# A graph layer on one core: order by sets of two units, 24 groups gathered wholly by TensorE, and another way to h's bf16 parts

## The chip, the cores and the metric

The kernel runs on one core of one Trainium2 chip. The metric is the device time of one execution in microseconds (us). Five engines work side by side, each through its own queue in order: TensorE (PE, with its weight loads as PEld), VectorE (DVE), ScalarE (ACT), GpSimd (POOL), and SyncE (SP), which here only issues DMA transfers.

## What is computed

One layer of a graph network with 6250 nodes of 64 values and 206250 edges, sorted by target node:

```
h   = relu(layernorm(x))                      # 6250 x 64
msg = relu(h[src] + edge_attr)                # 206250 x 64
agg = segment_sum(msg, dst)                   # 6250 x 64
out = x + relu((h + agg) @ W1 + b1) @ W2 + b2
```

## The kernel before

**Groups.** The edges are cut into 269 groups of 768: 128 partitions with G = 6 edges each (the last group has fewer). Because edges are sorted by target, all targets of a group lie in a window of W = 32 nodes. For each group the kernel needs the 768 rows h[src], adds the edge rows `ea`, takes the relu (`messages`, L589 to L605), and multiplies by a one-hot matrix `oh` of the edges' places in the window (`one_hot`, L577; `window_sum`, L607, two column halves of TensorE at a time). The result, 64 values by 32 nodes, is added into `z`, which holds h plus agg with the 64 values as partitions (`sum_into_z`, L573). Blocks of 512 nodes that are complete go through the two dense layers (`hidden`, `result`, `store`, L626 to L653).

**Two ways to h[src].** Half of a group's rows (three of its six columns) are gathered by GpSimd, one indirect DMA of 128 rows for each column (`gather`, L200, from the DRAM copy `h_rows`). The other half, a *unit* of 3 columns by 128 edges, comes from TensorE: h stands in SBUF as `hp`, 128 partitions by 49 node rows, as three bf16 parts whose sum is h in f32. TensorE first moves the wanted rows into slots (`slots_of`, L488, with the one-hot `found`) and then from the slots to the edges (`pick`, L508, with the one-hot `backs`), accumulating over `ea`, which ScalarE has put into the PSUM bank before (`room`, L517). A *whole* group has both halves from TensorE, so two units and no gather. The first F0 = 5 groups are gathered wholly, and the first RAW = 3 of them from x itself, with a layer norm of their own (`norm_edges`, L543), because h isn't ready by then.

**Units and sets.** The list `UNITS` (L65) has 276 units: 264 for groups 5 to 268, and 12 second ones for the whole groups (`WHOLE`, L64). Two units are a *set* (138), three sets a *chunk* (46). For every set, `find` (L460) makes `found` by two long compares and a short one on VectorE; `back_far`, `back` and `back_near` (L472 to L486) make `backs`, six compares of which VectorE does five and ScalarE the sixth (as a distance and a relu); `slots_out` (L505) evacuates the slots as bf16. For every chunk, the ranking steps `rank_at`, `rank_count`, `rank_of`, `rank_marks`, `rank_holds`, `rank_fits`, `rank_turn` and `source` (L278 to L347) sort the edges of six units into slots and write two small lists to DRAM, which SP loads again, spread over all partitions (`source_load`, `spot_load`).

**Order.** The order is written by hand; nothing reorders it. `half(u)` (L678) emits one unit: window sum of unit u - 1, room and slots for the next set (three pairs of slots), pick of unit u + 1, the messages of unit u, its one-hot, compares for later sets, the sum into z of unit u - 2, blocks, and at fixed distances the chunk steps. So TensorE's stream for a unit is W (window sum), S (slots), P (pick). `beats` are TensorE instructions that a gather waits for, so that gathers don't run ahead. Every 16 groups, `window_start` (L439) loads window positions into VectorE's registers.

**Opening.** The layer norm runs in four pieces over the 49 rows (`ln_head`, `ln_rows`, L356 to L377). After each piece TensorE transposes it into z (`ln_turn`, L379, evacuated by ScalarE). `slots_of_edges` (L741) computes all places in windows; it needs one small product by TensorE (L747). `ln_parts` (L389) makes the three bf16 parts of h with ScalarE and VectorE; it is a generator, and `fill` hands out its steps between the first five groups.

Of the kernel before, what the change touches and what calls it, by code (L numbers as in the profile page):

```python
# [21 lines left out]
G = 6  # L22
# [39 lines left out]
HEAD, PERIOD = 2 * RG - 1, 4 * RG - 1  # L62
assert (NG + 1 - F0 - HEAD) % PERIOD == 0
WHOLE = [F0 + RG - 1] + list(range(F0 + HEAD + 2 * RG - 1, NG + 1, PERIOD))  # L64
# [17 lines left out]
def kernel(  # L82
# [78 lines left out]
    nc.gpsimd.iota(from0, pattern=[[1, S], [0, H]], base=0, channel_multiplier=0, allow_small_or_imprecise_dtypes=True)  # L161
    ident_b = const.tile([P, P], BF16, name="ident_b")
    nc.vector.tensor_copy(ident_b, ident)
    ones_b = const.tile([P, P], F16, name="ones_b")
# [73 lines left out]
    code = const.tile([P, NCH, CC], F32, name="code")  # L238
    assert PARTS <= S

    def from0_all(n):
        return from0[:, :n].unsqueeze(1).to_broadcast([P, RG, n, H])
# [4 lines left out]
    def stretches(t_sb, c0, c1):  # L247

        n, g0 = (HEAD, F0) if c0 == 0 else (PERIOD, F0 + HEAD + (c0 - 2) // 4 * PERIOD)
# [5 lines left out]
    def places(c0, c1):  # L255
# [5 lines left out]
        own = lnp.tile([P, n, CC], F32, name="own", bufs=1)  # L261
        m, parts = stretches(src_sb, c0, c1)
        for src, w, gs in parts:
            nc.vector.tensor_copy(own.rearrange("p c s -> p (c s)")
                                  .rearrange("p (e w g j) -> p e w g j", w=2, g=m, j=H)[:, :, w, gs], src)
# [6 lines left out]
        nc.vector.scalar_tensor_tensor(part[:, c0:c1], off, float(RR), third, op0=ALU.add, op1=ALU.add)  # L272
        nc.vector.tensor_scalar(code[:, c0:c1], part[:, c0:c1], float(STEP), float(BIAS), op0=ALU.mult, op1=ALU.add)
# [4 lines left out]
    def rank_at(c):  # L278
        ats[c] = rank.tile([P, RG, PARTS, H], F16, name="at")
        nc.vector.tensor_tensor(ats[c], over(part[:, c], PARTS), from0_all(PARTS), ALU.is_equal)  # L280
# [12 lines left out]
    def rank_of(c):  # L293
# [7 lines left out]
        nc.vector.tensor_tensor(spot_i[c], ranks[c], code[:, c], ALU.add)  # L301
# [9 lines left out]
    def rank_holds(c):  # L311
        holds[c] = rank.tile([P, RG, S, H], F16, name="holds")
        nc.vector.tensor_tensor(holds[c], over(ranks[c], S), from0_all(S), ALU.is_equal)  # L313
# [41 lines left out]

    def ln_head(r, n):  # L356
# [32 lines left out]
    def ln_parts(r, m, h):  # L389
        hv = hp[:, r:r + m]  # L390
        rest = lnp.tile([PP, m, D], F32, name="rest")
        nc.scalar.copy(hv[:, :, 0], h)
        yield
        nc.vector.tensor_tensor(rest, h, hv[:, :, 0], ALU.subtract)
        nc.scalar.copy(hv[:, :, 1], rest)
        yield
        nc.vector.tensor_tensor(hv[:, :, 2], rest, hv[:, :, 1], ALU.subtract)
# [62 lines left out]

    def find(k, b):
# [3 lines left out]
        nc.vector.tensor_scalar(found[k][:, b * PARTS:b * PARTS + n].rearrange("p m i s -> p (m i s)"),  # L465
                                sources[k][:, :n * 2 * S], nodes_of[:, b:b + 1], None, op0=ALU.is_equal)

    far = const.tile([P, 1], F32, name="far")
    nc.vector.tensor_scalar_mul(far, ids[:, Q - 1:], -1.0)
    dists = {}  # L470

    def back_far(k):  # L472
        dists[k] = rank.tile([P, 2 * H * P], BF16, name="dist", bufs=1)
        nc.scalar.activation(dists[k], spots[k].bitcast(I16), AF.Abs, bias=far)  # L474

    def back_near(k):
        nc.scalar.activation(backs[k][:, Q - 1].rearrange("p t s -> p (t s)"), dists.pop(k), AF.Relu,  # L477
                             bias=ones[:, 0:1], scale=-1.0)
# [64 lines left out]
    def norm_edges(xg):  # L543
        s = work.tile([P, G], F32, name="raw_s")
# [5 lines left out]
        fill()  # L550
        v = work.tile([P, G], F32, name="raw_v")
        nc.vector.tensor_reduce(v, sq, AX.X, ALU.add)
        nc.scalar.activation(v, v, AF.Sqrt, bias=eps_sb, scale=1.0 / D)
        fill()
# [5 lines left out]
    pick_banks = [psum.tile([P, H + 1, 4, D], F32, name=f"pick{i}", bufs=1) for i in range(2)]  # L560

# [28 lines left out]
    def messages(u):  # L590
# [3 lines left out]
        if g < RAW:  # L594
            norm_edges(xg)
# [78 lines left out]

    def half(u):
        g = group_of(u)
        k, i = divmod(u, 2)
        first = ((0, 2), (6, 8))[i]  # L678
        later = ((4,), (10,))[i]
        now = is_set(k + 1)  # L680
        if is_first(u):
            enter(g + AHEAD, beats[-G + H:])
        if i == 0:
            if is_set(k + 3):
                source_load(k + 3)
        elif is_set(k + 3):
            spot_load(k + 3)
        window_sum(u - 1)
        if u + 1 < U:
            room(u + 1)  # L690
        if now:
            for n0 in first:
                begun = slots_of(k + 1, n0)
                slots_out(k + 1, n0)
                if n0 == first[0]:
                    beats.append(begun)
            for n0 in later:
                beats.append(slots_of(k + 1, n0))
        if u + 1 < U:
            beats.append(pick(u + 1, range(H)))  # L700
        messages(u)
        if now:
            for n0 in later:
                slots_out(k + 1, n0)
# [223 lines left out]
```

## Time and profile before

| | |
|---|---|
| Median of 3 runs | 1082.63 us (1082.12 to 1085.3) |
| The profiled execution, its own time | 1080.78 us |
| Its span | 1079.1 us |
| Granted TensorE clock, mean | 0.974 |
| Matmuls (PE) | 23185 |
| VectorE instructions | 2686 |
| ScalarE instructions | 1979 |

The profile is of one execution. A row of a timeline has the start, the time from the first start to the last end, the engine, the line of the kernel, the operation, its tiles (out<-in), shape and count; in brackets stands the idle time ahead of it and what ended it. A row of a group has the count, the busy time of all, the mean of one in ns, and the idle time ahead of them. Matmuls overlap, so their pace is read from start to start.

### The profile page before, as it was taken

What the parts mean: (1) busy time and instruction counts of PE and PEld (TensorE: products, weight loads), DVE (VectorE), ACT (ScalarE), POOL (GpSimd) and SP (SyncE); (2) the same over time, 40 slices, a digit from 0 to 9 for tenths busy, and PEclk for the clock granted to TensorE, in tenths of its full rate; (3) what the DMA queues carried; (4) which work ended last, traced back from release to release, by engine and by line L of the source; (5) the groups of instructions that cost most, each with busy time, mean ns of one, the idle gap of its engine ahead of it and who ended that gap; (6) DMA issues with size and microseconds to landing.
All of it is one profiled execution on the core that took longest, in us unless ns stands there. A gap on an engine that the chain in (4) does not pass through costs nothing.

```text
span 1079.1 us, 55140 instructions
## 1 busy us (share of the span) xinstructions
PE 994.9 (92%) x23185; PEld 865.5 (80%) x23185; DVE 960.5 (89%) x2686; ACT 940.6 (87%) x1979; POOL 793.9 (74%) x798
## 2 busy tenths in 40 slices
PE   3159999999999999999999999999999999999997
PEld 2148888888878888888888888888888888888885
DVE  8869889898998998998999898998999898998984
ACT  6459889899989998898998998998998998998985
POOL 7677777777777777777777777777777777777740
PEclk9659999999999999999999999999999999999998
DMA  6445566565655665665665656565656665655650
GB/s 207 126 117 150 164 164 187 141 178 158 188 143 150 180 190 143 170 169 165 163 174 149 184 157 165 155 199 156 161 148 187 164 170 154 185 158 161 167 132 10
DMA packets 115098, 172.36 MB, mean 160 GB/s; under 512 B 28444, under 2 KB 83613, under 8 KB 114845
## 3 DMA queue, kind: packets, MB, share of 16 engines
q1 hardware_dynamic: 89752, 143.03, 43.7%
q0 software_dynamic: 25088, 25.74, 13.5%
q8 instruction: 184, 3.01, 1.1%
q14 instruction: 70, 0.57, 0.2%
q10 hardware_dynamic: 4, 0.01, 0.0%
HBM read 164.85 MB, written 3.84 MB: 156 GB/s over the span
## 4 chain that ended last, share of the span: by engine, by line
PE 76%; DVE 10%; issue 5%; DMA 4%; ACT 3%; POOL 1%; DVEq 1%; SPq 0%; ACTq 0%
PE pick L513 34%; PE half L497 26%; PE half L612 10%; DVE backs L484 2%; DVE found L465 2%; DVE ea L600 2%; DMA xg<-h_rows,src_sb 2%; PE rows L339 2%; PE rows L642 1%; PE rows L631 1%; PE rows L287 1%; POOL xr L204 1%; DMA x<-in_x_dram 1%; DVE oh L581 1%; PE rows L285 1%
## 5 line engine op out<-in xcount | busy, mean ns | idle before, releaser
L204 POOL DMA_INDIRECT xg<-h_rows,src_sb x754 | 759.4, 1007 | 231.6 <-issue 105.2
L513 PE MATMUL pick<-picked,backs 128*128 128x192 bf16 x4968 | 459.9, 247 | 1.1 <-ACT pick L522 1.1
L513 PEld LDWEIGHTS <-backs 128*128 128x128 bf16 x4968 | 397.5, 98 | 45.1 <-issue 43.6
L506 ACT CAST picked<-half 128x384 bf16<-128x384 f32 x828 | 370.4, 480 | 54.3 <-PE half L497 47.2
L497 PE MATMUL half<-hp,found 128*32 128x192 bf16 x14352 | 352.8, 248 | 7.5 <-DVE found L465 4.9
L497 PEld LDWEIGHTS <-found 128*32 128x32 bf16 x14352 | 286.6, 97 | 22.2 <-issue 5.1
L484 DVE TENSOR_SCALAR backs<-spots,ids 128x768 bf16<-128x768 int16 x690 | 255.8, 419 | 0.0
L600 DVE TENSOR_REDUCE ea<-pick 128x192 f32<-128x576 f32 x276 | 206.8, 749 | 21.6 <-PE pick L513 19.7
L465 DVE TENSOR_SCALAR found<-sources,nodes_of 128x1536 bf16<-128x1536 int16 (+1 forms) x414 | 206.1, 525 | 0.1
L612 PEld LDWEIGHTS half<-oh,msg 128*64 128x64 f32 x3224 | 121.7, 138 | 62.0 <-issue 27.4
L522 ACT COPY pick<-ea 128x576 f32<-128x576 f32 x264 | 170.4, 646 | 0.0
L612 PE MATMUL half<-oh,msg 128*64 128x32 f32 x3224 | 152.4, 227 | 13.5 <-DVE z L575 10.8
L602 ACT ACTIVATE msg<-ea 128x384 f32<-128x384 f32 (+2 forms) x281 | 146.3, 521 | 10.7 <-DVE ea L600 7.2
L477 ACT ACTIVATE backs<-dist,ones 128x768 bf16<-128x768 bf16 x138 | 131.7, 954 | 0.3 <-ACT dist L474 0.3
L474 ACT ACTIVATE dist<-spots,far 128x768 bf16<-128x768 int16 x138 | 131.4, 952 | 0.0
L575 DVE TENSOR_TENSOR z<-z,half 128x32 f32 x281 | 50.9, 181 | 73.2 <-ACT picked L506 43.5
L581 DVE TENSOR_TENSOR oh<-slot,slots 128x192 f32<-128x192 int16 (+2 forms) x281 | 94.5, 336 | 1.0 <-PE half L612 1.0
L597 DVE TENSOR_TENSOR ea<-ea,xg 128x192 f32<-128x192 f32 x252 | 87.4, 347 | 0.7 <-issue 0.7
L285 PE MATMUL rows<-at,upper 128*128 128x432 f16 x46 | 16.4, 358 | 21.7 <-DVE at L280 19.7
L339 PE MATMUL rows<-holds,marks 128*96 128x96 f16 x276 | 25.8, 231 | 11.4 <-DVE holds L313 5.0
L291 ACT CAST before<-rows 128x432 f16<-128x432 f32 x46 | 23.9, 519 | 14.3 <-PE rows L287 14.3
L344 ACT CAST source<-rows 24x64 int16<-24x64 f32 x138 | 28.1, 203 | 9.5 <-PE rows L339 4.4
(107 smaller groups left out, 435.1 us busy)
## 6 DMA issues: line engine op xcount, KB each, us to landing
sources<-source_row SPq DMA_DIRECT2D x138, 384.0 KB
ea<-in_edge_attr_dram SPq DMA_DIRECT2D x268, 192.0 KB
spots<-spot_rows SPq DMA_DIRECT2D x138, 192.0 KB
xg<-h_rows,src_sb POOLq DMA_INDIRECT x754
xb<-in_x_dram SPq DMA_DIRECT2D x12, 128.0 KB
out_dram<-o SPq DMA_DIRECT2D x12, 128.0 KB
h_rows<-x SPq DMA_DIRECT2D x3, 384.0 KB
dst_sb<-in_dst_main_dram SPq DMA_DIRECT2D x1, 804.0 KB
```

Of the source, the lines that this page charges most:

```text
L204: it = nc.gpsimd.indirect_dma_start(out=xg[:, j, :], out_offset=None, in_=rows[:, :], in_offset=bass.IndirectOffsetOnAxis(ap=idx[:, j:j + ...
L465: nc.vector.tensor_scalar(found[k][:, b * PARTS:b * PARTS + n].rearrange("p m i s -> p (m i s)"), sources[k][:, :n * 2 * S], nodes_of[:, b ...
L474: nc.scalar.activation(dists[k], spots[k].bitcast(I16), AF.Abs, bias=far)
L477: nc.scalar.activation(backs[k][:, Q - 1].rearrange("p t s -> p (t s)"), dists.pop(k), AF.Relu, bias=ones[:, 0:1], scale=-1.0)
L484: nc.vector.tensor_scalar(backs[k][:, q].rearrange("p t s -> p (t s)"), spots[k].bitcast(I16), ids[:, q:q + 1], None, op0=ALU.is_equal)
L497: last = nc.tensor.matmul(ps[j * S:(j + 1) * S, u], found[k][:, m, i, :], hp[:, min(m, RR - 1)].rearrange("p t d -> p (t d)"), start=(b == ...
L506: nc.scalar.copy(picked[k][:, n0:n0 + 2], halves.pop((k, n0)))
L513: last = nc.tensor.matmul(ps[:, u, :3].rearrange("p t d -> p (t d)"), backs[k][:, q, i * H + u, :], picked[k][:, i * Q + q], start=False, ...
L522: nc.scalar.copy(picks[u][:, :H, :3], parts)
L600: nc.vector.tensor_reduce(ea[:, c0:c0 + H], picks.pop(u)[:, :H, :3].rearrange("p j t d -> p j d t"), AX.X, ALU.add)
L602: nc.scalar.activation(msg[:, lo:hi], ea[:, lo:hi], AF.Relu)
L612: last = nc.tensor.matmul(pa[i * D:(i + 1) * D], msg[:, j, :], oh[:, j, :], start=(j < lo + 2), stop=(j >= hi - 2))
```

## The change

- **24 whole groups.** `WHOLE` has every eleventh group instead of every 23rd: 24 instead of 12. That is 288 units, 144 sets and 48 chunks, and 718 gathers instead of 754 in the loop.
- **Order by sets.** `half` has two shapes. For the first unit of a set: window sum of unit u - 1, room, the first three pairs of slots with their evacuations, pick of u + 1, messages, room for u + 2, one-hot, both sums into z, blocks, the last three compares of `backs`, the first of `found`. For the second: pick of u + 1, messages, the other three pairs of slots, window sum of u - 1, one-hot, the first three compares of `backs`, the second of `found`. So TensorE's stream for a set is W, W, S, P, P, S instead of W, S, P, W, S, P. The chunk steps stand one unit earlier; those of TensorE fall between the two P.
- **Compares.** All six compares of `backs` are VectorE's; the short one of `found` is ScalarE's, as a distance and a relu.
- **h's bf16 parts.** TensorE subtracts: into PSUM goes h by the identity (f32), less the first part by a negative identity (bf16); ScalarE evacuates the difference as the second part, TensorE takes that off too, and ScalarE evacuates the third. This is done within the layer norm, piece by piece.
- **Transposes.** All four `ln_turn` stand behind the layer norm and the parts, ahead of `slots_of_edges`.
- **Raw groups.** Their layer norm is done step by step for the three groups together.
- **Places.** The constant of `code` is part of `part`, so `code` goes; the casts of the later chunks' source numbers are ScalarE's, within the layer norm.

```diff
-HEAD, PERIOD = 2 * RG - 1, 4 * RG - 1
-WHOLE = [F0 + RG - 1] + list(range(F0 + HEAD + 2 * RG - 1, NG + 1, PERIOD))
+HEAD = PERIOD = 2 * RG - 1
+WHOLE = list(range(F0 + RG - 1, NG + 1, PERIOD))
...
-        nc.vector.tensor_scalar(code[:, c0:c1], part[:, c0:c1], float(STEP), float(BIAS), op0=ALU.mult, op1=ALU.add)
...
-    def ln_parts(r, m, h):
-        hv = hp[:, r:r + m]
-        rest = lnp.tile([PP, m, D], F32, name="rest")
-        nc.scalar.copy(hv[:, :, 0], h)
-        yield
-        nc.vector.tensor_tensor(rest, h, hv[:, :, 0], ALU.subtract)
-        nc.scalar.copy(hv[:, :, 1], rest)
-        yield
-        nc.vector.tensor_tensor(hv[:, :, 2], rest, hv[:, :, 1], ALU.subtract)
+    def mid_piece(i, r, m, h):
+        hv = hp[:, r:r + m]
+        nc.scalar.copy(hv[:, :, 0], h)
+        for ps, rows_of in pieces(i, r, m):
+            nc.tensor.matmul(ps, ident, h[:, rows_of].rearrange("p r d -> p (r d)"), start=True, stop=False)
+            nc.tensor.matmul(ps, less_b, hv[:, rows_of, 0], start=False, stop=True)
+        flat = pick_banks[i % 2].rearrange("p j t d -> p (j t) d")
+        nc.scalar.copy(hv[:, :, 1], flat[:, :m])
+
+    def low_piece(i, r, m, h):
+        hv = hp[:, r:r + m]
+        for ps, rows_of in pieces(i, r, m):
+            nc.tensor.matmul(ps, less_b, hv[:, rows_of, 1], start=False, stop=True, skip_group_check=True)
+        flat = pick_banks[i % 2].rearrange("p j t d -> p (j t) d")
+        nc.scalar.copy(hv[:, :, 2], flat[:, :m])
...
+        if b < BB:
+            nc.vector.tensor_scalar(to, sources[k][:, :n * 2 * S], nodes_of[:, b:b + 1], None, op0=ALU.is_equal)
+        else:
+            dist = rank.tile([P, J * 2 * S], BF16, name="dist", bufs=1)
+            nc.scalar.activation(dist, sources[k][:, :n * 2 * S], AF.Abs, bias=last_node)
+            nc.scalar.activation(to, dist, AF.Relu, bias=ones[:, 0:1], scale=-1.0)
...
-        for q in range(q0, min(q1, Q - 1)):
+        for q in range(q0, q1):
...
+        if i == 0:
             window_sum(u - 1)
             room(u + 1)
+            if is_set(k + 1):
+                slots_by(k + 1, (0, 2, 4))
             beats.append(pick(u + 1, range(H)))
+            messages(u)
+            if u + 2 < U:
+                room(u + 2)
+            one_hot(u)
+            for v in (u - 2, u - 1):
+                sum_into_z(v)
+                blocks_behind(v)
             if is_set(k + 1):
                 back(k + 1, 3, Q)
             if is_set(k + 2):
                 find(k + 2, 0)
                 find(k + 2, BB)
         else:
+            if u + 1 < U:
+                beats.append(pick(u + 1, range(H)))
+            messages(u)
+            if is_set(k + 1):
+                slots_by(k + 1, (6, 8, 10))
+            window_sum(u - 1)
+            one_hot(u)
             if is_set(k + 2):
                 back(k + 2, 0, 3)
+                find(k + 2, 1)
...
         if len(rows) > 1:
-            ln_turn(*rows[-2])
+            low_piece(len(rows) - 2, *rows[-2])
+        if rows:
+            mid_piece(len(rows) - 1, *rows[-1])
...
+        if r == CUTS[3]:
+            own = places_own(2, NCH)
     rows.append(ln_rows(*heads[-1]))
-    ln_turn(*rows[-2])
-    split = [ln_parts(*r) for r in rows]
+    low_piece(len(rows) - 2, *rows[-2])
+    mid_piece(len(rows) - 1, *rows[-1])
+    low_piece(len(rows) - 1, *rows[-1])
+    for row in rows:
+        ln_turn(*row)
...
     slots_of_edges()
-    ln_turn(*rows[-1])
...
+    for step in (raw_head, raw_var, raw_rows):
+        for g in range(RAW):
+            step(g)
```

More of the change, by code (lines that the diff above doesn't have):

```diff
@@ L354, in next_half @@
         return half_banks[halves_made[0] % 3]
+    pick_banks = [psum.tile([P, H + 1, 4, D], F32, name=f"pick{i}", bufs=1) for i in range(2)]
     def ln_head(r, n):
@@ L464, in find @@
         n = PARTS if b < BB else J
[L465 to L478, printed above, removed]
+        to = found[k][:, b * PARTS:b * PARTS + n].rearrange("p m i s -> p (m i s)")
+        if b < BB:
+            nc.vector.tensor_scalar(to, sources[k][:, :n * 2 * S], nodes_of[:, b:b + 1], None, op0=ALU.is_equal)
+        else:
+            dist = rank.tile([P, J * 2 * S], BF16, name="dist", bufs=1)
+            nc.scalar.activation(dist, sources[k][:, :n * 2 * S], AF.Abs, bias=last_node)
+            nc.scalar.activation(to, dist, AF.Relu, bias=ones[:, 0:1], scale=-1.0)
     def back(k, q0, q1):
@@ L541, in span, with raw_head @@
         return first_col(g), G
-    def norm_edges(xg):
-        s = work.tile([P, G], F32, name="raw_s")
+    raw = {}
+    def raw_head(g):
+        xg = taken[g][1]
+        s = work.tile([P, G], F32, name="raw_s", bufs=RAW)
         nc.vector.tensor_reduce(s, xg, AX.X, ALU.add)
@@ L673, in is_set, with slots_by @@
         return 0 <= k < KS
+    def slots_by(k, n0s):
+        for n0 in n0s:
+            last = slots_of(k, n0)
+            slots_out(k, n0)
+            if n0 != n0s[1]:
+                beats.append(last)
     def half(u):
@@ L758 @@
     heads, rows = [], []
-    places(0, 2)
+    places(0, 2, places_own(0, 2))
     rank_at(0)
@@ L787 @@
         enter(g)
-    places(2, NCH)
+    places(2, NCH, own)
     for k in (0, 1):
@@ L818 @@
     sum_into_z(-LAG - 1)
-    while split:
-        fill()
     ln_stack.close()
```

120 lines of the change are left out of this document (51 added, 69 removed).

## The prediction

> **What bounds the kernel now.** I read the page's busy shares and its chain first, then one window over the whole edge loop, then TensorE's timeline inside it.
>
> ```profile
> span 1079.1 us, 55140 instructions
> ...
> PE 994.9 (92%) x23185; PEld 865.5 (80%) x23185; DVE 960.5 (89%) x2686; ACT 940.6 (87%) x1979; POOL 793.9 (74%) x798
> ...
> PE 76%; DVE 10%; issue 5%; DMA 4%; ACT 3%; POOL 1%; DVEq 1%; SPq 0%; ACTq 0%
> ```
> ```profile
> 78.00:1065.00 987.00, 962.18 (x22873) 841.87 (x22871) 896.28 (x2536) 894.16 (x1896) 736.52 (x731) 1.00 0.60 162
> ```
> The columns of the window are its length and the busy time of PE, PEld, DVE, ACT, POOL. The edge loop (unit 0's window sum to the last unit's) takes 987 of 1079 us; TensorE idles 24.8 us of it, VectorE 90.7. So three things count: TensorE's work per set, how near VectorE comes to it, and the 78 us ahead of the loop.
>
> **The loop on TensorE.** Three units, L513 being the pick P, L612 the window sum W, L497 the slots S:
>
> ```profile
> 502.29 1.66 PE L513 MATMUL pick<-picked,backs 128*128 128x192 bf16 x18
> 503.79 0.56 PE L339 MATMUL rows<-holds,marks 128*96 128x96 f16 x6
> 504.27 0.54 PE L612 MATMUL half<-oh,msg 128*64 128x32 f32 x12
> 504.74 1.26 PE L497 MATMUL half<-hp,found 128*32 128x192 bf16 x52
> 505.93 1.66 PE L513 MATMUL pick<-picked,backs 128*128 128x192 bf16 x18
> 507.52 0.54 PE L612 MATMUL half<-oh,msg 128*64 128x32 f32 x12
> 507.99 1.26 PE L497 MATMUL half<-hp,found 128*32 128x192 bf16 x52
> 509.18 1.66 PE L513 MATMUL pick<-picked,backs 128*128 128x192 bf16 x18
> 510.68 0.35 PE L285 MATMUL rows<-at,upper 128*128 128x432 f16 x1
> 510.86 0.47 PE L287 MATMUL rows<-at,ones_b 128*128 128x288 f16 x2
> 511.26 0.42 PE L612 MATMUL half<-oh,msg 128*64 128x32 f32 x6
> 511.61 1.26 PE L497 MATMUL half<-hp,found 128*32 128x192 bf16 x52
> ```
> From start to start: a unit is 505.93 to 509.18 = 3.25 us, a set 6.50. P takes 1.59 ahead of W but 1.50 ahead of L339 or L285, so leaving P for the 64-column W costs 0.09. W with 12 matmuls takes 0.47, with 6 (half a group) 0.35: 0.12 for 6, so 0.25 for 12 and 0.22 for coming and going.
>
> The new order of a set is W W S P P S: six changes of kind become four. P P takes 1.50 + 1.59 = 3.09. The two S take 2.38, if P to S and S to W, which this trace doesn't show, cost what the shown changes do. The first W of the pair takes at least 0.25 (no change) and at most 0.35; with 0.30 the pair is 0.77. The set: 3.09 + 2.38 + 0.77 = 6.24 (6.19 to 6.29; with two free changes about 6.0). The Trainium skill, TensorEngine Tiling (Array Packing), Key Properties, says that changing the tiling mode drains TensorE; by that rule both unseen changes drain, the upper values hold, and the 0.09 above agrees. Now 288 units are 144 sets: 144 x 6.24 = 899 against 138 x 6.50 = 897: +2 (-5 to +9). Twenty-four more units have the short W: -3.
>
> Ranking steps (46 chunks, then 48) now all stand between two P's. Today L285/L287 add 0.58 - 0.09, L339 0.48 - 0.09, and L325 0.16:
>
> ```profile
> 84.42 0.22 PE L325 MATMUL rows<-ident_b,spot_i 128*18 128x128 bf16 x1
> 84.58 0.54 PE L612 MATMUL half<-oh,msg 128*64 128x32 f32 x12
> ```
> Sum 1.04. Between P's the change W would have needed isn't shared any more: 0.50 + 0.40 + 0.25 = 1.15 (1.0 to 1.25). Per chunk +0.1, and two chunks more: +7 (0 to +12). TensorE in all: +6 (-8 to +18), so 968 us busy.
>
> **The loop on VectorE.** Here the sixth compare of backs comes from ScalarE, and the short compare of found goes to it.
>
> ```profile
> L484 DVE TENSOR_SCALAR backs<-spots,ids 128x768 bf16<-128x768 int16 x690 | 255.8, 419 | 0.0
> L600 DVE TENSOR_REDUCE ea<-pick 128x192 f32<-128x576 f32 x276 | 206.8, 749 | 21.6 <-PE pick L513 19.7 <-ACT msg L602 0.9
> L465 DVE TENSOR_SCALAR found<-sources,nodes_of 128x1536 bf16<-128x1536 int16 x276 | 174.6, 633 | 0.1
> L465 DVE TENSOR_SCALAR found<-sources,nodes_of 128x256 bf16<-128x256 int16 x138 | 42.5, 308 | 0.0
> L477 ACT ACTIVATE backs<-dist,ones 128x768 bf16<-128x768 bf16 x138 | 131.7, 954 | 0.3 <-ACT dist L474 0.3
> L474 ACT ACTIVATE dist<-spots,far 128x768 bf16<-128x768 int16 x138 | 131.4, 952 | 0.0
> L602 ACT ACTIVATE msg<-ea 128x256 f32<-128x256 f32 x1 | 0.4, 403 | 0.0
> ```
> backs: 864 - 690 = 174 more, 255.8/690 = 0.37 each: +64. Short found: -42.5. Twelve more reduces +9, twelve more long founds +7.6; two chunks of about 2.5 us +5; the other small ones cancel. VectorE +44: 940 us. ScalarE loses 263 us of 768-wide passes and gains 288 of about 0.45, 130 us, so from 894 it falls to about 760 and gives no bound. Every 16 groups VectorE also loads window starts into registers and stands still:
>
> ```profile
> 250.87 0.19 DVE L575 TENSOR_TENSOR z<-z,half 128x32 f32 x1 [2.14 <-ACT dist L474]
> PE half L612 <- DVE z L575: 9.2, 12, 1.4
> ```
> The first row is one such stop (2.14 us idle; the releaser named was long done), the second what TensorE waits behind them today: 9.2 us in all, since VectorE runs ahead by over 1 us. 940 + 15 x 2.1 = 972: VectorE's own floor passes TensorE's 968. In the new order these stops stand between z and the three backs that the second P waits for, and behind them in VectorE's queue are found, the next reduce, and so ScalarE's room and relu. I let them cost 9 us more than now, and take 9 off for waits that go because ranking's inputs are a set old: TensorE's idle stays 25. Loop: 968 + 25 = 993, **+6** (-8 to +30).
>
> **Ahead of the loop.** VectorE's way to the loop, with the rows that price the new steps:
>
> ```profile
> 14.83 1.02 DVE L372 SCALAR_TENSOR_TENSOR x<-x,ln_v 128x832 f32<-128x832 f32 x1
> 26.61 0.96 DVE L372 SCALAR_TENSOR_TENSOR x<-x,ln_v 128x768 f32<-128x768 f32 x1
> 28.92 1.83 DVE L748 SCALAR_TENSOR_TENSOR slot<-dst_sb,rows 128x1608 int16<-128x1608 int32 x1 [0.87 <-PE rows L747]
> 68.27 1.34 DVE L465 TENSOR_SCALAR found<-sources,nodes_of 128x1536 bf16<-128x1536 int16 x3
> L394 DVE TENSOR_TENSOR rest<-x,hp 128x768 f32<-128x768 f32 x3 | 2.9, 968 | 0.2 <-ACT hp L392 0.2
> L397 DVE TENSOR_TENSOR hp<-rest,hp 128x768 bf16<-128x768 f32 x3 | 2.9, 952 | 0.9 <-ACT hp L395 0.9
> L392 ACT CAST hp<-x 128x768 bf16<-128x768 f32 x3 | 2.4, 815 | 0.0
> L363 ACT ACTIVATE ln_sq<-x 128x768 f32<-128x768 f32 x3 | 2.5, 843 | 6.9 <-DVE x L361 4.9 <-issue 2.0
> L387 ACT COPY z<-half 64x512 f32<-64x512 f32 x12 | 6.8, 644 | 1.6 <-PE half L386 1.6
> L631 PE MATMUL rows<-z,w_sb 128*64 128x512 f32 x24 | 12.9, 618 | 1.5 <-DVE z L575 1.5
> 15.91 2.77 PE L386 MATMUL half<-ident,x 128*64 128x128 f32 x12 [0.55 <-DVE x L372]
> 28.81 1.50 PE L386 MATMUL half<-ident,x 128*64 128x128 f32 x12
> ```
> From slot at 28.92 to the first found at 68.27 are 39.4 us of VectorE. What goes: eight L394/L397 (about 7.4 laid end to end), the casts of own and code (1.3), some 3 of waits between raw groups; ranking's third chunk comes in (+1.1). About **30 remain**.
>
> But slot waits for a product (L747) that stood ahead of the last 12 transposes and now stands behind all 49, and these behind the whole split of h. ScalarE's queue ties the layer norm to the split: hp's copy, the evacuation of TensorE's difference, the next Square and Sqrt. One piece: L372 0.96, difference of 768 columns in f32 (512 are two records of L631, so up to 1.9) plus 0.3 in bf16, evacuation 0.83, Square 0.84, Sqrt and reciprocal 0.55, hand-overs 0.3: 5.6 us against (26.61 - 14.83)/3 = 3.9. Three steps: +5, and ranking's small evacuations stand in the first: +2. The norm ends at 34.6 instead of 27.6; the last piece's copies and differences take 4: 38.6. Then 13 evacuations of transposes at about 0.55; the product follows the last transposes, which need the tenth evacuation: 38.6 + 5.6 + 1.2 = 45.4. With TensorE at the slower pace (12 transposes in 2.77 instead of 1.50) it is 51. I take 46.5, nearer to the fast one. The Trainium skill, TensorE: Matmul & The Clock Gate, Part 1, has the clock halve only after an idle window of about 3.4 us; by that rule the gaps here (some 2 us) keep it fast and 45.4 holds; today's 2.77 ahead of 1.50 agrees with a warm-up. First found: 46.5 + 30 = 76.5 against 68.3: **+8** (+5 to +13). Behind slot in VectorE's queue stand places, raw groups, messages; nothing else can use that time. SP's queue keeps its order (stores of h, weights, edge rows, then sources and spots), 7 us later with the norm. The gathers of h start 7 us later, too: POOL needs 730 x 1.31 = 956 from about 38, done by 994, long ahead of the last unit.
>
> **Sum.** 1080.8 (this execution: 1079.1 and 1.7 around it) + 6 + 8 = 1095; the median of the runs shown, 1082.6, lies 1.9 above it, so 1095 to 1097. I say **1096**.
>
> **Rivals.**
> 1. Faster: TensorE's switches. If P to S and S to W cost nothing and ranking nothing more, TensorE does 954, with VectorE ahead enough to hide its stops (25 idle become 15): 969, -18; with the opening at +6: 1069. It decides if a set takes under 6.1 us. For it: 0.09 measured at P. Against: VectorE's 972. 13%.
> 2. POOL sets the pace now:
> ```profile
> L204 POOL DMA_INDIRECT xg<-h_rows,src_sb x754 | 759.4, 1007 | 231.6 <-issue 105.2 <-PE half L497 55.7 <-PE pick L513 16.5
> ```
> Then 36 gathers less, at (759.4 + 231.6)/754 = 1.31, take 47 off: 1042 with the opening. Against: half of its idle follows TensorE's beats, and the chain has 1% POOL. 4%.
> 3. VectorE becomes the bound: 972 plus 35 to 50 us of waits that it can't lose because reduces follow picks: loop 1007 to 1022, time 1109 to 1124. It decides when TensorE's idle passes 45 us. 18%.
> 4. The opening isn't longer (TensorE and ScalarE overlap more than I laid end to end) while the loop is level: 1079 to 1086. 13%.
> My forecast, 1086 to 1110: 52%.
>
> Range: 1074 to 1116, rivals 2 and the ends of 1 and 3 left out. About 0.3% (3.2 us) is what a measurement of this kernel can tell from no change. Faster 0.17, same 0.13, slower 0.70.
>
> **What would show it.** Slot at 45 or later and first found at 74 to 79; loop sets near 6.7 us with ranking; P following P after 1.50; VectorE over 940 us in the loop and idle only at register loads; POOL done 30 us before the end. Wrong if slot comes before 38, if W after S needs no change, or if TensorE idles over 45 us in the loop.

## The result and the profile after

The changed kernel takes **1161.3 us** (median of 4, 1158.4 to 1162.03) against 1083.97 for the kernel before beside it (median of 4, 1082.12 to 1086.61): ratio 1.071, 95% interval 1.067 to 1.074, so 77 us more. The profiled execution took 1162.03 us, its span is 1160.3. The prediction said 1096, 1074 to 1116: the sign was right, the size far too small.

First the edge loop in one window, from its first window sum to 8 us ahead of the end of its last (length, busy PE, PEld, DVE, ACT, POOL, granted clock, DMA share, GB/s):

```profile
90.00:1145.00 1055.00, 1000.73 (x23676) 879.08 (x23673) 945.56 (x2632) 829.46 (x1985) 702.28 (x694) 0.98 0.58 155
```

The loop begins 13 us later (at 90.9 instead of 77.8) and lasts 1055 us in this window, against 987 in the prediction's window of the kernel before. VectorE's 945.56 us are what was forecast (940). TensorE idles 54 us instead of 25, and its clock is 0.98 instead of 1.00: 2% of 1055 is 21 us of lost pace, from eleven stretches at half clock in the trace's clock records (41 us in all; the kernel before has one, of 3.4 us).

A set, in TensorE's timeline (L518 is slots, L534 pick, L636 window sum, L295/L297 and L335 ranking):

```profile
504.17 0.89 PE L636 MATMUL half<-oh,msg 128*64 128x32 f32 x24
504.99 1.26 PE L518 MATMUL half<-hp,found 128*32 128x192 bf16 x52
506.18 1.66 PE L534 MATMUL pick<-picked,backs 128*128 128x192 bf16 x18
507.68 0.35 PE L295 MATMUL rows<-at,upper 128*128 128x432 f16 x1
507.86 0.47 PE L297 MATMUL rows<-at,ones_b 128*128 128x288 f16 x2
508.14 1.67 PE L534 MATMUL pick<-picked,backs 128*128 128x192 bf16 x18
509.74 1.26 PE L518 MATMUL half<-hp,found 128*32 128x192 bf16 x52
510.99 0.77 PE L636 MATMUL half<-oh,msg 128*64 128x32 f32 x18
511.68 1.26 PE L518 MATMUL half<-hp,found 128*32 128x192 bf16 x52
```

From 504.99 to 511.68 it is 6.69 us; the next, with L335 as its ranking step, takes 6.41, so 6.25 without that step's 0.16. Both have a short pair of window sums, of 18 matmuls. With 24 matmuls, which the forecast of 6.24 was made for, a set with L335 takes 6.53 at the least, so 6.37. That is about 0.1 us more than forecast; the 77 us are elsewhere. I sorted the sets by what happens in them (from start to start of the slots, medians, by the trace's rows):

| | before: sets, us | after: sets, us |
|---|---|---|
| plain | 109, 6.89 | 116, 6.67 |
| with a block of 512 nodes | 11, 9.06 | 10, 10.75 |
| with a register load | 16, 7.68 | 15, 9.33 |

One more set after has both (11.86). A plain set became 0.22 shorter. A block costs 4.1 us over a plain set instead of 2.2, a load 2.7 instead of 0.8. Six sets are new, and the opening is longer. The waits in the loop tell the same (us in total, times, longest), first of TensorE, then of VectorE:

```profile
PE pick L534 <- DVE backs L505: 24.5, 15, 3.0
PE rows L666 <- ACT h L658: 8.5, 11, 0.8
```
```profile
DVE z L601 <- issue: 28.0, 8, 3.6
DVE z L601 <- PE rows L655: 24.8, 10, 3.7
```

TensorE's fifteen waits for backs go with the register loads, the eleven for h with the blocks. A set with a block, on both engines:

```profile
439.08 1.07 PE L655 MATMUL rows<-z,w_sb 128*64 128x512 f32 x2
440.93 1.10 PE L666 MATMUL rows<-w_sb,h 64*128 64x64 f32 x8 [0.77 <-ACT h L658]
442.49 0.34 PE L295 MATMUL rows<-at,upper 128*128 128x432 f16 x1 [0.46 <-ACT o L668]
442.67 0.47 PE L297 MATMUL rows<-at,ones_b 128*128 128x288 f16 x2
442.95 2.88 PE L534 MATMUL pick<-picked,backs 128*128 128x192 bf16 x18
```
```profile
437.49 0.18 DVE L601 TENSOR_TENSOR z<-z,half 128x32 f32 x1
440.19 0.19 DVE L601 TENSOR_TENSOR z<-z,half 128x32 f32 x1 [2.52 <-PE rows L655]
440.30 1.12 DVE L505 TENSOR_SCALAR backs<-spots,ids 128x768 bf16<-128x768 int16 x3
```

The first sum completes the block. The new `half` calls `blocks_behind` at once, so `hidden` (L655) reads z ahead of the second sum, which must wait for it, and L655 itself stands in TensorE's queue behind a pick. The compares that the second pick needs follow 2.5 us late; and because `blocks_behind` is called again in the same half, `result` (L666) follows at once and TensorE waits for ScalarE twice. Then the pick runs at half clock: 2.88 instead of 1.66 us.

In the opening the slot's product waits for all 49 transposes, and these for the split of h, whose last three steps on TensorE run at half clock (by the clock records from 23.4 to 47.3 us):

```profile
37.01 0.96 DVE L384 SCALAR_TENSOR_TENSOR x<-x,ln_v 128x768 f32<-128x768 f32 x1
51.74 1.83 DVE L764 SCALAR_TENSOR_TENSOR slot<-dst_sb,rows 128x1608 int16<-128x1608 int32 x1 [13.30 <-PE rows L763]
81.28 1.31 DVE L495 TENSOR_SCALAR found<-sources,nodes_of 128x1536 bf16<-128x1536 int16 x2
```
```profile
38.02 2.08 PE L412 MATMUL pick<-x,ident 128*128 128x512 f32 x2 [1.78 <-DVE dst_sb L760]
43.07 7.99 PE L398 MATMUL half<-ident,x 128*64 128x128 f32 x49
```

The norm ends 10.4 us later than before, slot comes 22.8 later, found 13.0 later: 9.8 us less remain behind slot, as forecast (39.4 before, 29.5 now).

### The profile page after: what moved, and what is told of

It is laid out like the page before. It is cut to its first block, busy times and chain, and to the rows that moved or that the text cites. A ratio compares the mean times of both kernels' runs of the same rounds, so it can differ in the third digit from the quotient of the medians.

```text
span 1160.3 us, 56720 instructions
## 1 busy us (share of the span) xinstructions
PE 1050.4 (91%) x24077; PEld 909.7 (78%) x24077; DVE 1002.0 (86%) x2772; ACT 881.3 (76%) x2080; POOL 759.5 (65%) x763
## 5 line engine op out<-in xcount | busy, mean ns | idle before, releaser
L209 POOL DMA_INDIRECT xg<-h_rows,src_sb x718 | 726.4, 1012 | 331.5 <-PE half L518 109.9
L534 PE MATMUL pick<-picked,backs 128*128 128x192 bf16 x5184 | 497.5, 250 | 29.0 <-DVE backs L505 24.5
L534 PEld LDWEIGHTS <-backs 128*128 128x128 bf16 x5184 | 428.9, 99 | 70.9 <-DVE backs L505 36.2
L518 PE MATMUL half<-hp,found 128*32 128x192 bf16 x14976 | 372.8, 251 | 4.7 <-DVE found L495 2.4
L518 PEld LDWEIGHTS <-found 128*32 128x32 bf16 x14976 | 304.5, 98 | 36.4 <-issue 27.1
L505 DVE TENSOR_SCALAR backs<-spots,ids 128x768 bf16<-128x768 int16 x864 | 318.1, 422 | 0.7 <-DMA spots<-spot_rows 0.7
L626 ACT ACTIVATE msg<-ea 128x384 f32<-128x384 f32 (+1 forms) x293 | 148.6, 507 | 103.6 <-DVE ea L624 99.3
L495 DVE TENSOR_SCALAR found<-sources,nodes_of 128x1536 bf16<-128x1536 int16 x288 | 177.0, 615 | 0.0
L636 PEld LDWEIGHTS half<-oh,msg 128*64 128x64 f32 x3224 | 111.2, 140 | 36.2 <-ACT picked L527 30.9
L636 PE MATMUL half<-oh,msg 128*64 128x32 f32 x3224 | 127.9, 227 | 8.7 <-ACT picked L527 5.9
L607 DVE TENSOR_TENSOR oh<-slot,slots 128x192 f32<-128x192 int16 (+1 forms) x293 | 96.1, 328 | 6.0 <-PE half L636 6.0
L499 ACT ACTIVATE found<-dist,ones 128x256 bf16<-128x256 bf16 x144 | 73.2, 508 | 4.7
L498 ACT ACTIVATE dist<-sources,last_node 128x256 bf16<-128x256 int16 x144 | 74.4, 517 | 0.0
L295 PE MATMUL rows<-at,upper 128*128 128x432 f16 x48 | 17.3, 360 | 27.6 <-DVE at L290 22.5
L308 DVE TENSOR_REDUCE rank_of<-before 128x18 f16<-128x432 f16 x48 | 28.9, 603 | 1.6
```

Source lines behind the costliest of these rows:

```text
L209: it = nc.gpsimd.indirect_dma_start(out=xg[:, j, :], out_offset=None, in_=rows[:, :], in_offset=bass.IndirectOffsetOnAxis(ap=idx[:, j:j + ...
L495: nc.vector.tensor_scalar(to, sources[k][:, :n * 2 * S], nodes_of[:, b:b + 1], None, op0=ALU.is_equal)
L505: nc.vector.tensor_scalar(backs[k][:, q].rearrange("p t s -> p (t s)"), spots[k].bitcast(I16), ids[:, q:q + 1], None, op0=ALU.is_equal)
L518: last = nc.tensor.matmul(ps[j * S:(j + 1) * S, u], found[k][:, m, i, :], hp[:, min(m, RR - 1)].rearrange("p t d -> p (t d)"), start=(b == ...
L534: last = nc.tensor.matmul(ps[:, u, :3].rearrange("p t d -> p (t d)"), backs[k][:, q, i * H + u, :], picked[k][:, i * Q + q], start=False, ...
L607: nc.vector.tensor_tensor(oh[:, lo:hi], slot[:, g * G + lo:g * G + hi].unsqueeze(2).to_broadcast([P, n, W]), slots.unsqueeze(1).to_broadca ...
```

## The experiments

**Theory A**: the time goes into the opening, into blocks whose steps meet in one half, and into register loads for which VectorE has no lead any more. **Theory B**, the main rival (the prediction's third): VectorE, with the sixth compare, bounds every set, and waits taken away only move. Each ratio is to the kernel before on the same chip; the changed kernel's is 1.071, and 0.001 is 1.1 us.

**The opening of before** in the changed kernel:

```diff
-            low_piece(len(rows) - 2, *rows[-2])
-        if rows:
-            mid_piece(len(rows) - 1, *rows[-1])
+            ln_turn(*rows[-2])
...
+    split = [ln_parts(*r) for r in rows]
...
     slots_of_edges()
+    ln_turn(*rows[-1])
```

> The changed kernel with the opening of the kernel before: h's parts by ScalarE and VectorE handed out between the raw groups, transposes within the layer norm, the small product ahead of the last transposes. Theory A (what the trace of the changed kernel shows: 13 us lost in the opening, the rest in single sets of the loop): the slot row falls from 51.7 to about 30, the first found comes at 67 to 70 instead of 81, the time falls by 11 to 15, to about 1148. Theory B (the later start is mostly absorbed, because VectorE sets the pace of the whole loop and the loop then merely starts earlier and waits more): less than 5 us.

Measured 1146.8 us, ratio 1.060 (1.057 to 1.064), 11 to 15 less. Slot and first found:

```profile
29.74 1.83 DVE L757 SCALAR_TENSOR_TENSOR slot<-dst_sb,rows 128x1608 int16<-128x1608 int32 x1 [1.41 <-PE rows L756]
67.92 1.31 DVE L482 TENSOR_SCALAR found<-sources,nodes_of 128x1536 bf16<-128x1536 int16 x2
```

Found comes 13.4 us earlier and the whole gain arrives at the end: the loop is not a fixed pace that absorbs a later start. Theory A.

**The slots of the edges ahead of the transposes**, the split staying where the change put it:

```diff
-    for row in rows:
-        ln_turn(*row)
...
     slots_of_edges()
+    for row in rows:
+        ln_turn(*row)
```

> The changed kernel with the slots of the edges (and their small product) ahead of the 49 transposes instead of behind them; the split stays in the layer norm. Theory A1 (of the 14 us that the opening lost, the transposes ahead of the product cost more than the split): the slot row comes at 38 to 42 instead of 51.7, the first found at 70 to 74, the time falls by 7 to 11. Rival A2 (the split and the 13 evacuations hold the raw groups anyway): first found at 78 or later, less than 4.

Measured 1151.6 us, ratio 1.062 (1.060 to 1.065), 9 to 10 less:

```profile
43.59 1.83 DVE L764 SCALAR_TENSOR_TENSOR slot<-dst_sb,rows 128x1608 int16<-128x1608 int32 x1 [5.09 <-PE rows L763]
73.70 1.27 DVE L495 TENSOR_SCALAR found<-sources,nodes_of 128x1536 bf16<-128x1536 int16 x2
```

The slot comes 1.6 us later than the expected 38 to 42; found comes 7.6 us earlier. So more than half of the opening's 13 us is the product behind the transposes; the split within the norm keeps the other 5.8 (73.70 against 67.92).

**Blocks apart**: both sums first, then one pass, so that `hidden`, `result` and `store` fall in three sets:

```diff
-    def blocks_behind(u):
+    def blocks_behind(*us):
...
             for v in (u - 2, u - 1):
                 sum_into_z(v)
-                blocks_behind(v)
+            blocks_behind(u - 2, u - 1)
```

> The changed kernel with both sums into z first and one pass over the blocks behind them, so that hidden, result and store of a block of 512 nodes fall into three different sets. Theory A: the 11 sets with a block take 10.75 us in the median against 6.67 of the plain ones, +4.1 each, where the kernel before has +2.2; apart they fall to +2 or so, 15 to 25 us less in all, 1136 to 1146. Theory B (VectorE is the bound, waits only move): the block sets shrink but plain sets grow, less than 6 us.

Measured 1146.8 us, ratio 1.060 (1.057 to 1.062), 12 to 15 less. Block sets fall from 10.75 to 8.69, plain sets stay at 6.67. The 24.8 us of z waiting for L655 are gone; the same block now:

```profile
432.26 1.07 PE L655 MATMUL rows<-z,w_sb 128*64 128x512 f32 x2
434.11 0.34 PE L295 MATMUL rows<-at,upper 128*128 128x432 f16 x1 [0.77 <-ACT h L658]
```

What waits (0.77) is the ranking step, which shares the bank `rows` with `hidden`. Theory A, just under its low end (15). The block sets alone lost 11 x 2.06 = 23 us; where the rest went shows in the starts of the slots, from this block's set on:

```profile
429.48 1.26 PE L518 MATMUL half<-hp,found 128*32 128x192 bf16 x52
438.18 1.26 PE L518 MATMUL half<-hp,found 128*32 128x192 bf16 x52
446.32 1.26 PE L518 MATMUL half<-hp,found 128*32 128x192 bf16 x52
453.36 1.25 PE L518 MATMUL half<-hp,found 128*32 128x192 bf16 x52
```

The set with `hidden` takes 8.70 us, the one with `result` 8.14, the one with `store` 7.04. Plain sets with the same ranking steps and window sums take 6.76, 6.53 and 6.66. So a block still costs 3.9 us, spread over three sets.

**Small register loads**, of 2 window starts instead of 16:

```diff
-RV = 16
+RV = 2
```

> The changed kernel with register loads of 2 window starts instead of 16: a load of 16 holds VectorE's queue 3.61 us, of 13 2.95, of 1 0.33, so 0.22 for each start; of 2 it should be about 0.55, at 8 times as many places. Theory A: the 16 sets with a load (9.33 us in the median, +2.7 over a plain set) become plain ones, because 0.55 us run ahead of VectorE's work; 25 to 40 us less, 1121 to 1136. Theory B (VectorE is the bound, and the 59 us of loads stay on it, spread): less than 8 us.

Measured 1118.6 us, ratio 1.032 (1.030 to 1.035), 41 to 43 less, just past theory A's end. VectorE's work is the same (944.87 us from 87 to 1101), so B falls here: the same work, in 41 us less. The loop's window and what is left of z's stops:

```profile
87.00:1101.00 1014.00, 986.29 (x23690) 870.97 (x23692) 944.87 (x2633) 827.92 (x1985) 713.24 (x695) 0.99 0.59 161
```
```profile
DVE z L601 <- issue: 5.3, 16, 0.5
```

The longest is 0.5 instead of 3.6, and no pick waits for backs any more. Of the 41 us TensorE's waits for backs are 24.5. The clock can be up to 12: five half-clock stretches instead of eleven, 17 us instead of 41, half of it lost. The rest isn't broken down.

**All compares of backs half a set earlier**, loads of 16:

```diff
         if i == 0:
...
-            if is_set(k + 1):
-                back(k + 1, 3, Q)
             if is_set(k + 2):
                 find(k + 2, 0)
                 find(k + 2, BB)
+                find(k + 2, 1)
         else:
...
-                back(k + 2, 0, 3)
-                find(k + 2, 1)
+                back(k + 2, 0, Q)
...
-    back(1, 0, 3)
+    back(1, 0, Q)
```

> The changed kernel with all six compares of backs in the second half of a set (a half earlier for three of them) and both long compares of found in the first half; register loads of 16 and blocks as in the change. Theory A (a load or a block costs so much because the three compares that the second pick waits for stand just behind the sums into z in VectorE's queue): load sets fall from 9.33 to 7.5 us or so, the row of TensorE's pick waiting for backs from 24.5 us to under 8, the time by 20 to 40, 1121 to 1141. Rival C (a stop of 3.6 us costs the same wherever the compares stand, since reduce and the one-hot stand behind it as well): less than 10.

Measured 1155.3 us, ratio 1.069 (1.064 to 1.074): no difference that can be told from the change. A miss for A. The pick waits for backs no more, but the stop came back one step later, at the window sum. TensorE's largest wait, then one case of it on TensorE and on VectorE:

```profile
PE half L636 <- ACT picked L527: 23.9, 16, 2.3
```
```profile
202.45 1.23 PE L636 MATMUL half<-oh,msg 128*64 128x32 f32 x18 [2.03 <-ACT picked L527]
```
```profile
198.92 0.19 DVE L601 TENSOR_TENSOR z<-z,half 128x32 f32 x1 [3.57 <-issue]
...
200.72 0.75 DVE L624 TENSOR_REDUCE ea<-pick 128x192 f32<-128x576 f32 x1
```

The view names ScalarE's `picked`, which was long done; the window sum needs the relu of what the reduce makes, and the reduce, 200.72 to 201.47, stands behind the load. Load sets fall only to 8.48. So the place of the three compares isn't the cause; a stop of 3.6 us on an engine without lead is, wherever it stands. Rival C was right.

**The same small loads in the kernel before** (the same line changed, nothing else):

> The kernel before with register loads of 2 window starts instead of 16, nothing else. Theory A (the loads cost there only what VectorE's lead doesn't hide: load sets 7.68 us against 6.89): 8 to 16 us less, 1067 to 1075, against 43 in the changed kernel. Rival D (they cost as much in both kernels, and the change isn't to blame for them): 30 or more less, 1050.

Measured 1067.7 us, ratio 0.985 (0.983 to 0.987): 16 less, the end of A's range, and faster than both kernels. So the loads were a cost before, too, and the change made it 2.6 times as large.

**The opening of before, blocks apart and small loads together** (the three diffs above):

> The changed kernel with three changes at once: the opening of before, blocks apart, register loads of 2. Theory A (three separate causes): the gains add up, 14 + 14 + 43 = 71 less, 1084 to 1096, plain sets 6.67 us and hardly any half-clock stretch in the loop. Theory B (a common bound takes over): 1100 or more.

Measured 1094.6 us, ratio 1.011 (1.008 to 1.014). By the ratios each alone takes 11, 12 and 41, which makes 64; all three in one kernel take 65: they add up.

```profile
74.66:1085.37 1010.71, 983.42 (x23794) 868.90 (x23793) 947.84 (x2640) 830.41 (x1993) 716.81 (x699) 1.00 0.60 162
```

This is the whole loop, from its first window sum to the end of the last. The clock is 1.00 again and TensorE idles 27 us, near the forecast 25. The prediction's window of the kernel before ends 5 us ahead of the last window sum, so its 968 busy and 993 long are 973 and 998 here: TensorE's work is 10 us more than forecast, the loop 12.

**The new order alone on the kernel before:**

```diff
...
+            for v in (u - 2, u - 1):
+                sum_into_z(v)
+                blocks_behind(v)
             if is_set(k + 1):
                 back_near(k + 1)
                 back(k + 1, 3, Q)
-            sum_into_z(u - LAG)
-            blocks_behind(u - LAG)
...
```

> The kernel before with the new order of a set alone (W W S P P S, the ranking steps a unit earlier); 12 whole groups, the opening, the sixth compare on ScalarE and the short compare on VectorE stay as before. Theory A: plain sets 0.22 us shorter (109 of them, 24 us less), block sets 21 us and load sets 30 us more together, so 20 to 35 us more than the kernel before, 1104 to 1119. Theory B (the sixth compare on VectorE is what made the loop longer, so the order without it gains the switches): no more than the kernel before, 1060 to 1085.

Measured 1190.2 us, ratio 1.098 (1.095 to 1.101). Both theories missed: plain sets take 7.48 us. I formed A': the sixth compare on ScalarE is what the order P P can't bear. Of what this kernel keeps from before, that compare is what lies within every plain set. So I put **the sixth compare back on ScalarE** (and the short one of found on VectorE) in the kernel with the three repairs:

```diff
             if is_set(k + 1):
+                back_near(k + 1)
                 back(k + 1, 3, Q)
...
             if is_set(k + 2):
+                back_far(k + 2)
                 back(k + 2, 0, 3)
...
-        for q in range(q0, q1):
+        for q in range(q0, min(q1, Q - 1)):
```

> The kernel with the opening of before, blocks apart, loads of 2, 24 whole groups and the sixth compare on ScalarE, a third time. If the kernel before takes about 1083 beside it: Theory A' (ScalarE's 1.9 us stand between the two picks): plain sets 7.3 to 7.6 us, 1175 to 1210. Theory B (the sixth compare on VectorE is a burden): 1085 or less.

Measured 1195.2 us, ratio 1.104 (1.101 to 1.107), plain sets 7.48: A', and the opposite of B. Two compares were moved together here; which of them stands in the way is read from the trace. Timelines of TensorE and ScalarE in one set:

```profile
510.13 0.57 PE L525 MATMUL pick<-picked,backs 128*128 128x192 bf16 x5 [0.19 <-DVE found L477]
511.00 1.25 PE L525 MATMUL pick<-picked,backs 128*128 128x192 bf16 x13 [0.29 <-ACT backs L489]
```
```profile
508.79 0.55 ACT L617 ACTIVATE msg<-ea 128x384 f32<-128x384 f32 x1
509.22 0.34 ACT L536 COPY pick<-ea 128x192 f32<-128x192 f32 x1
509.60 0.48 ACT L537 COPY pick<-ea 128x384 f32<-128x384 f32 x1
510.01 0.93 ACT L489 ACTIVATE backs<-dist,ones 128x768 bf16<-128x768 bf16 x1
```

Between the two picks ScalarE has a relu, the room for the second pick (L536, L537) and then the compare (L489) to do, and the second pick waits for both: it starts behind L537, though the view names found, and stops again until L489 is done. In the changed kernel, where VectorE makes all six, a pick waits for backs only behind register loads.

**Twelve whole groups** again, with the three repairs:

```diff
-HEAD = PERIOD = 2 * RG - 1
-WHOLE = list(range(F0 + RG - 1, NG + 1, PERIOD))
+HEAD, PERIOD = 2 * RG - 1, 4 * RG - 1
+WHOLE = [F0 + RG - 1] + list(range(F0 + HEAD + 2 * RG - 1, NG + 1, PERIOD))
```

> The kernel with the opening of before, blocks apart, register loads of 2 and 12 whole groups, a third time: the first two runs fell to chips on which TensorE's instructions come slower and the kernel before takes 1430 to 1453 us. If the kernel before takes about 1083 beside it: Theory A (TensorE's work per set is the bound, the 6 added sets cost their whole length): 1051 to 1058, 40 less than the 1094.6 with 24 whole groups. Rival (GpSimd near its bound): over 1070.

Measured 1073.2 us, ratio 0.991 (0.988 to 0.994): 21 less than with 24, half of what A said; the rival, over 1070, was right, if by a little. The profiled execution was the slowest of five, 1083.9 us, so its totals lie above the median's. GpSimd's largest waits in its loop (us in total, times, longest) and what VectorE now waits for:

```profile
POOL xg L209 <- issue: 76.5, 251, 0.3
POOL xg L209 <- PE half L505: 47.2, 155, 0.3
```
```profile
DVE ea L608 <- DMA xg<-h_rows,src_sb: 9.5, 7, 2.4
```

The third column never passes 0.3, in no row of that view: each gather follows the last after that time, whatever is named, so GpSimd runs without a wait. Its 754 gathers take 1012 us with these gaps (1.04 us busy on the mean), against 991 in the kernel before (1.01); why they take longer isn't shown. The kernel before shows nearly the same waits (a few up to 1.1 aside):

```profile
POOL xg L204 <- issue: 97.6, 320, 0.3
POOL xg L204 <- PE half L497: 54.5, 173, 1.1
```

In the changed kernel the first row is a real wait, up to 7.3 us:

```profile
POOL xg L209 <- PE half L518: 101.8, 166, 7.3
```

So 24 whole groups do free GpSimd, and pay for it with six sets of TensorE. With 12 the kernel before with small loads is still 5.6 us faster (1067.7); there GpSimd never waits over 0.3 either, so these two can't tell what the new order is worth.

**Runs on two other chips.** Three of these kernels came first to chips on which the kernel before takes 1453.5 and 1429.1 us. They are the kernel with 12 whole groups, the same with early backs (both diffs above), and the one with the sixth compare on ScalarE:

> The three changes of the run before last taken together (opening of before, blocks apart, register loads of 2) and 12 whole groups again instead of 24: 276 units, 138 sets, 754 gathers. Theory A (TensorE's work per set is the bound, so the 6 sets that the change added cost their whole length): 6 x 6.67 = 40 us less than with 24 whole groups, 1051 to 1058. Rival (GpSimd is near the bound, and 36 gathers more at 1.0 us busy and 0.1 of issue each set it): over 1070.

> As the run with 12 whole groups, and all six compares of backs a half earlier. Theory A (with loads of 2 nothing stands late ahead of backs any more): within 4 us of that run, either way. Rival C (some plain and block sets still wait for backs): 5 to 15 us less.

> The changed kernel with opening of before, blocks apart, loads of 2 and 24 whole groups, but the sixth compare of backs on ScalarE and the short one of found on VectorE, as before. Theory A' (formed when the order alone on the kernel before gave 1190 us: between the two picks ScalarE's 1.9 us for the sixth compare stand in the way, so the compares' move is what lets the new order keep 6.67 us a set): plain sets 7.3 to 7.6 us, 80 to 115 us more than with the sixth compare on VectorE, 1175 to 1210. Theory B (the sixth compare on VectorE is a burden): 1085 or less.

Measured 1468.6 (ratio 1.010), 1454.8 (1.001) and 1495.9 us (1.029). On the second chip:

> The kernel with the opening of before, blocks apart, register loads of 2 and 12 whole groups once more, since the first run fell to a chip on which the kernel before takes 1453.5 us and TensorE stops for 0.45 us every few matmuls. On a chip on which the kernel before takes about 1083: Theory A (TensorE's work per set is the bound, the 6 added sets cost their whole length): 6 x 6.67 = 40 us less than the 1094.6 with 24 whole groups, 1051 to 1058. Rival (GpSimd near its bound): over 1070.

> The same with all six compares of backs a half earlier, once more. Theory A: within 4 us of the run with 12 whole groups beside it. Rival C (some sets still wait for backs): 5 to 15 us less.

> The kernel with the opening of before, blocks apart, loads of 2, 24 whole groups and the sixth compare on ScalarE, once more. Theory A' (ScalarE's 1.9 us stand between the two picks): plain sets 7.3 to 7.6 us, 80 to 115 us more than 1094.6, so 1175 to 1210. Theory B (the sixth compare on VectorE is a burden): 1085 or less.

Measured 1447.0 (1.011), 1433.6 (1.002) and 1486.4 us (1.040). TensorE stops within a run of slots, for nothing that the profile shows (here 12 whole groups, on the first of the two chips):

```profile
706.55 0.32 PE L505 MATMUL half<-hp,found 128*32 128x192 bf16 x5 [0.46 <-issue]
707.31 0.32 PE L505 MATMUL half<-hp,found 128*32 128x192 bf16 x5 [0.43 <-issue]
```

So these six runs tell nothing of the question put to them. Early backs with small loads gained 0.9% there in both cases; on a chip like the first it wasn't tried.

## Why the prediction was wrong

- **TensorE's work per plain set: right, to 0.1 us.** With ranking 6.62 was forecast; sets with 24 matmuls in the pair of window sums take 6.53, 6.66 and 6.76 at the least, by their ranking step, 6.65 on the mean. P P after 1.50 is confirmed, and the two unseen changes of kind do cost: P to S 1.60 (509.74 - 508.14) against 1.50 where the kind stays, and the pair of window sums 0.82 (0.77 forecast). The Trainium skill, TensorEngine Tiling (Array Packing), Key Properties, says a changed tiling mode drains TensorE; these rows agree. No plain set took under 6.20, so the first rival (under 6.1) fell.
- **VectorE's work: right**, 946 against 940. ScalarE came to 829 instead of 760: each pass for the short compare takes 0.51 instead of 0.45, and the six new sets' other work on it was left out. It is no bound at 829 either.
- **"I let them cost 9 us more than now": the first step that failed.** The register loads cost 41 us in the changed kernel and 16 in the one before, so 25 more, not 9. I read the cost from TensorE's waits (9.2 us) and took the stop as the 2.14 us of VectorE's idle; but a load holds the queue 3.6 us, and the 2.14 was what VectorE's lead left of it. The prediction's own 940 + 15 x 2.1 = 972 already passed TensorE's 968, so no lead was left; with 3.6 it is 994.
- **The second, a term put at nothing:** two sums and two passes over the blocks in one half. It stood in the diff, as `blocks_behind(v)` in a loop over two units. I counted z's and the blocks' work and didn't ask what the second sum waits for. 12 us go with the blocks apart, and some 18 stay (below).
- **Also left out: the clock.** The sum ran TensorE at full clock; at 0.98, 21 us of pace go (no term beside the others: with all three repairs it is 1.00).
- **The opening: 13 us instead of 8, and partly luck.** I gave slot at 51 for transposes at the slow pace, and 51.74 it was, but by another step. The norm ended at 38.0 instead of 34.6 and the last parts at 44.1 instead of 38.6, since the differences ran at half clock: ScalarE waited 2.79 us for each of three, where the sum had at most 2.2. From there to slot it took 7.6 us, nearer to the fast pace (6.8) than to the slow one (12.4). The Trainium skill, TensorE: Matmul & The Clock Gate, Part 1, has the clock halve after an idle window of about 3.4 us; by that rule gaps of some 2 us keep it fast. In the opening a gap of 1.78 us (the L412 row above) stands beside the slow pace, and in the loop a pick ran at half pace behind gaps of 0.77 and 0.46: the measurement decides against reading the rule as a full window without work.
- **TensorE's idle "stays 25": wrong.** It is 54 (27 with the three repairs). That passes the third rival's point of decision (45), but its mechanism, VectorE as the bound of every set, is refuted: plain sets are shorter than before, small loads take 41 us off with the same work, and VectorE relieved of a compare gives 1195 us.
- **Rival 2 was dismissed on a misreading.** "Half of its idle follows TensorE's beats" took the named releaser for a wait (and it is 72 of 231.6 us in the row shown, a third). The idle time is 0.3 us behind each gather. GpSimd and TensorE were level in the kernel before. It still gave no gain, since TensorE was as near.

The account, 75 of the 77 us: 11 for the opening, 12 for the blocks, 25 for the loads beyond what they cost before (41 less 16). The remaining 27 are what the kernel with the three repairs (1094.6) takes more than the kernel before with small loads (1067.7), on one chip. The whole loop of the latter, beside the row of the former above:

```profile
77.63:1059.14 981.51, 966.47 (x22934) 845.25 (x22933) 901.44 (x2544) 894.80 (x1900) 732.40 (x733) 1.00 0.60 163
```

With the repairs the loop begins 3 us earlier and is 29 longer; TensorE is busy 17 us more, where +6 was forecast, and idles 12 more. By the starts of the slots, sets that are neither a block's own nor one of the two behind it take 6.71 us on the mean against 6.93. So six more cost 40 and the others save 0.22 each, 29 in all: 11 net, near the forecast. The other 18 are the blocks: each, with the two sets behind it, costs 4.1 us over such sets against 2.5, 45 us in all against 28. Together with the 12 that is 30 us for blocks, the largest term, and the prediction had nothing for it. Why blocks cost more in the new order even when they are apart, no run isolates.

## What to carry to other kernels

Before an order is packed tighter, look for the rare steps (a register load every 16 groups, a block every 12 sets): an average over all sets hides them, and what an engine's lead has paid for them is lost with the lead. Split a long stop into short ones where it can be split; that alone made the kernel before 1.5% faster. Read the longest wait beside the total: many waits of the same small length are a fixed cost of the instruction, not a wait for the one that is named.

## What the runs showed of the hardware

- A register load of window starts holds VectorE's queue in proportion: 3.60 us for 16, 2.95 for 13, 0.33 for 1, by the trace's records. One of 2 takes 0.51, and with those z's longest stop at one is 0.5.
- TensorE's half-clock stretches are 3.4 us long or a multiple of that (clock records), and a few gaps under 1 us were enough for one.
- An indirect DMA of 128 rows takes GpSimd 1.00 to 1.04 us on the mean and 0.3 us more until the next, whichever event the view names.
- Chips differ: the same kernel before takes 1083 us on some and 1429 or 1453 on two others, and a trace from one of these has stops of 0.43 to 0.46 us in TensorE's runs of slots. Ratios there are 1.001 to 1.011 for as many matmuls as before and 1.029 and 1.040 for 3.7% more; whether the count is the reason isn't shown.
